# Encoder-decoder layer on one core: the negated maxima of four heads made by one reduction, and the first query block's cross-attention normalization issued in two steps

## The chip, the cores and the metric

The kernel runs on one core of a Trainium2 chip. The core has five engines with a queue of instructions each, worked off in order: TensorE (PE in the profile, its weight loads PEld), VectorE (DVE), ScalarE (ACT), GpSimd (POOL) and SyncE (SP, which here issues the DMAs). The metric is device time in microseconds (us); several runs are given by their median.

## The reference

A pre-norm transformer layer with an encoder over a short context (2 x 77 rows of 512) and a decoder over 2 x 2048 rows of 512; 16 heads of 32, feed-forward width 2048. Cut to what matters:

```
def _mha(xq, xkv, w_in, b_in, w_out, b_out, bias):
    q, k, v = (x @ w.T + b, split into 16 heads of 32)
    scores = q @ k / sqrt(32) + bias[None]          # bias depends on key - query, per head
    attn = softmax(scores, axis=-1)
    return (attn @ v) @ w_out.T + b_out

x = src;  x = x + _mha(ln(x), ln(x), ..., eb);  x = x + relu(ln(x) @ ff1.T + b) @ ff2.T + b   # encoder, 77 rows
memory = x
y = tgt
y = y + _mha(ln(y), ln(y), ..., sb)                 # self attention, causal: 2048 rows see themselves and those before
y = y + _mha(ln(y), memory, ..., cb)                # cross attention: 2048 rows over 77 keys
y = y + relu(ln(y) @ ff1.T + b) @ ff2.T + b         # feed-forward
```

The softmax is computed with each row's maximum taken away before the exponential.

## The kernel before

The decoder rows of a batch b are cut in four blocks m of 512 rows, a block in four query blocks t of 128 rows. There are 4 groups g of 4 heads.

**First half: self attention.** A unit is (b, m, g, t): one query block and the four heads of one group; there are 128, worked in that order. With i = 4m + t a unit has i + 1 key tiles of 128, cut by `pieces` in pieces of up to four tiles. The code is an order written out by hand (the pool has `manual_schedule`): it interleaves, over a stream of pieces, five steps.

- `scores` (line 344): TensorE multiplies q by kT into four PSUM banks, one for each head (line 361). Then DVE goes head by head. Far keys are copied to `pp` with their maximum (line 370); in the last piece of a unit the two tiles at the diagonal get their bias and their maximum (line 377), and a small reduction over the partial maxima makes the negated maximum `nm` of this head (line 384). The exponential of a head (line 387, on ACT, with bias `nm`) is issued at once in block m = 0. In the others it is put in a list, `late_exps`, from which `exps` takes one or two at given places.
- `turn` (line 397): TensorE transposes the exponentials tile by tile (line 411) into PSUM banks; ACT (line 417) and DVE (line 415) copy one half each to `pts`.
- `slot`: the jobs of a unit, which are projections (lines 206, 217, 230, 242), norms, stages of the encoder in the first 30 units or so, and cross attention of the very first block (`first_cross`) in the first units of b = 1.
- `values` (line 422): `pts` times v (line 428).
- `divide`: division by the sums.

PSUM banks are handed out in a ring of seven by `bank()`, whoever asks. A bank is free again when the copy or the pass that reads it is done: a score bank by lines 370 and 377, a transpose's bank by lines 415 and 417. Scores run up to two units ahead of `turn`.

**Second half: cross attention and feed-forward.** For each of the 8 blocks there are 56 slots (`ff_slot`), 28 for each feed-forward layer, which is multiplied by seven products of four slots each. A slot first calls `prepare(s + 3)`, which makes the operand sums (line 1115) for the product three slots later, on POOL in layer 1, into a ring `w_ring` of four buffers; then TensorE multiplies (line 1132 in layer 1, line 1161 in layer 2), and DVE and ACT add the product up (lines 1145, 1147, 1150). Ahead of each slot one step of the generator `cross(x + 1)` runs, that is cross attention of the next block. Its stages come from `attend_stages` (line 754): score (TensorE line 766, DVE lines 773 to 776), exp (ACT line 779), normalize (sums `csu` line 784 and reciprocal `cri` line 785 on DVE, multiply line 786 on POOL), turned (transposes line 792), times_v, out. The places of the stages in `cross` are counted from at = 14 + 7t, by the list at line 1227:

```
for k, f in zip((0 if t else -1, 2 if t else 1, 3 if t else 2, 6, 9, 11), fs):
    plan[at + k].append(f)
```

So for t = 0 score is at slot 13, exp at 15, normalize at 16 and turned at 20.

Of the kernel before, what the change touches and what calls it, by code (L numbers as in the profile page):

```python
# [11 lines left out]
AF = mybir.ActivationFunctionType  # L12
ALU = mybir.AluOpType
AX = mybir.AxisListType
# [3 lines left out]
P = 128  # L18
# [4 lines left out]
HC = P // HD  # L23
# [31 lines left out]
def tile_encoder_decoder(ctx: ExitStack, tc: tile.TileContext, ins, out):  # L55
    nc = tc.nc
# [92 lines left out]
    with (  # L149
# [35 lines left out]
        nTs, qTs, ots, sums_of = {}, {}, {}, {}  # L185
# [151 lines left out]
        late_exps = []  # L337
# [6 lines left out]
        def scores(n, k0, kn):  # L344
            b, m, g, t = units[n]
            i = m * TB + t
            if k0 == 0:
                state[n] = {
                    "p": probabilities(n),
                    "mx": sm.tile([P, HC, 8], F32, name="mx", tag="mx"),  # L350
                    "nm": sm.tile([P, HC], F32, name="nm", tag="nm"),
                    "col": 0,
                }
                if t == 0:
                    sums_of[b, m, g] = sm.tile([P, TB, HC], F32, name="sums", tag="sums")
            st = state[n]
            last = k0 + kn == i + 1
            q = qTs[b, m, g]
            banks = [bank() for _ in range(HC)]
            for r in range(HC):  # L360
                nc.tensor.matmul(  # L361
                    banks[r][:, : kn * P], q[rows4(r), ts(t, P)], kT[rows4(r), g, k0 * P : (k0 + kn) * P],
                    start=True, stop=True,
                )
            far = max(0, kn - 2) if last else kn
            col = st["col"]
            for r in range(HC):
                p, s, c = st["p"][r], banks[r], col
                if far:
                    nc.vector.tensor_scalar(  # L370
                        p[:, k0 * P : (k0 + far) * P], s[:, : far * P], 1.0, None, ALU.mult, ALU.max,
                        accum_out=st["mx"][:, r, c : c + 1],
                    )
                    c += 1
                if last:
                    w = (kn - far) * P
                    nc.vector.tensor_tensor_reduce(  # L377
                        p[:, (i + 1) * P - w : (i + 1) * P], s[:, far * P : kn * P],
                        biases[b, m, g][:, r, 2 * P - w :], 1.0, LOWEST, ALU.add, ALU.max,
                        accum_out=st["mx"][:, r, c : c + 1],  # L380
                    )
                    c += 1
                    nm = st["nm"][:, r : r + 1]
                    nc.vector.tensor_reduce(nm, st["mx"][:, r, :c], AX.X, ALU.max, negate=True)  # L384

                    def run(p=p[:, : (i + 1) * P], nm=nm, to=sums_of[b, m, g][:, t, r : r + 1]):
                        nc.scalar.activation(p, p, AF.Exp, bias=nm, accum_out=to)  # L387

                    if m:
                        late_exps.append((n, run))  # L390
                    else:
                        run()
            st["col"] = c

        got = {}

# [357 lines left out]
        def attend_stages(q, kTc, v, y, biased, pr, pts, place, w_o, bi=None):  # L754


            prh = pr.rearrange("p (h k) -> p h k", k=S)
            by_r = pr.rearrange("p (g r k) -> p g r k", r=HC, k=S)
            keep = {}

            def score():
                mx = sm.tile([P, NC, HC], F32, name="cmx", tag="cmx", bufs=3)
                banks = [bank() for _ in range(HC)]
                for g in range(NC):
                    for r in range(HC):
                        nc.tensor.matmul(  # L766
                            banks[r][:, ts(g, S)], q(g)[rows4(r)], kTc[rows4(r), g, :], start=True, stop=True
                        )
                for r in range(HC):
                    s = banks[r][:, : NC * S].rearrange("p (g k) -> p g k", k=S)  # L770
                    d = by_r[:, :, r, :]
                    if biased:
                        nc.vector.tensor_tensor(d, s, bi[r] if bi else d, ALU.add)
                        s = d
                    nc.vector.tensor_reduce(mx[:, :, r], s, AX.X, ALU.max)
                    nc.vector.tensor_tensor(d, s, mx[:, :, r, None].to_broadcast([P, NC, S]), ALU.subtract)

            def exp():
                nc.scalar.activation(pr, pr, AF.Exp)

            def normalize():
                su = sm.tile([P, H], F32, name="csu", tag="csu", bufs=2)
                ri = sm.tile([P, H], F32, name="cri", tag="cri", bufs=2)
                nc.vector.tensor_reduce(su, prh, AX.X, ALU.add)
                nc.vector.reciprocal(ri, su)
                nc.gpsimd.tensor_tensor(prh, prh, ri[:, :, None].to_broadcast([P, H, S]), ALU.mult)

            def turned():
                for g in range(NC):
                    pt = bank()  # L790
                    for r in range(HC):
                        nc.tensor.transpose(pt[:S, ts(r, P)], prh[:, g * HC + r, :], ident)  # L792
                    if g % 2:
                        nc.vector.tensor_copy(pts(g), pt[:S, :])
                    else:
                        nc.scalar.copy(pts(g), pt[:S, :])

            def times_v():
                ot = bank()
                for g in range(NC):  # L800
                    for r in range(HC):
                        h = g * HC + r
                        nc.tensor.matmul(
                            ot[rows4(r), ts(g, P)], v[:, ts(h, HD)], pts(g)[:, ts(r, P)], start=True, stop=True
                        )
                keep["oT"] = place()
                nc.scalar.copy(keep["oT"], ot)

            def out():
                mm, oT = bank(), keep["oT"]  # L810
                for c in range(NC):
                    nc.tensor.matmul(mm, oT[:, ts(c, P)], w_o[:, c, :], start=(c == 0), stop=(c == NC - 1))  # L812
                nc.vector.tensor_tensor(y(), mm, y(), ALU.add)

            return score, exp, normalize, turned, times_v, out

        def first_cross():

# [40 lines left out]
            for t in range(TB):  # L859
                y = lambda t=t: ys[t]  # L860
                fs = norm_stages(
                    y, "n2", rows["dec_ca_out_b"], lambda: xn, lambda t=t: nT[:, :, ts(t, P)]
                )
# [4 lines left out]
            for t in range(TB):  # L868
                y = lambda t=t: ys[t]
                fs = attend_stages(  # L870
                    lambda g, t=t: qT[:, g, ts(t, P)], kTc, vc, y, t < 2, prs[t % 2], pts, lambda: oT, wo
                )
                for k, f in zip((0, 1, 2, 4, 5, 6), fs):
                    at(11 + 3 * t + k, f)
                fs = norm_stages(y, "n3", rows["dec_ff2_b"], lambda: xn, lambda: slab)
                for k, f in enumerate(fs):
                    at(18 + 3 * t + k, f)

                def store(t=t):
                    nc.sync.dma_start(nT3_d[:, :, ts(t, P)], slab)  # L880
                    nc.sync.dma_start(y1[0][0][:, t, :], ys[t])

                at(20 + 3 * t, store)
# [308 lines left out]
        def cross(x):  # L1192

            b, m = blocks[x]
# [7 lines left out]
            for t in range(TB):  # L1202
                fs = norm_stages(
                    lambda t=t: y_of(x, t), "n2", bv, place("xt"), lambda t=t: nT2[:, :, ts(t, P)]
                )
# [11 lines left out]
            for t in range(TB):  # L1217
                at = 14 + 7 * t
                y = lambda t=t: y_of(x, t)
                biased = m == 0 and t < 2  # L1220
                fs = attend_stages(
                    lambda g, t=t: qT[g // 2][:, g % 2, ts(t, P)], kTcs[b], vcs[b][:S, :], y, biased, pr,
                    lambda g: pts_all[:S, g, :], place("xr"), wbt,
                    bias_1 if biased and t else None,
                )

                for k, f in zip((0 if t else -1, 2 if t else 1, 3 if t else 2, 6, 9, 11), fs):
                    plan[at + k].append(f)
                fs = norm_stages(y, "n3", bo, place("xt"), lambda t=t: nTt[:, :, ts(t, P)])
                for k, f in zip((13, 15, 17), fs):  # L1230
                    plan[at + k].append(f)
# [29 lines left out]
        i = 0  # L1261
        while i < len(stream):
            n = stream[i][0]
# [97 lines left out]
```

## Time and profile before

| | |
|---|---|
| median of 3 runs | 2927.04 us (2926.18 to 2927.46) |
| profiled execution | 2926.58 us, its span 2924.8 us |
| TensorE busy | 2866.0 us, 98% of the span |
| VectorE busy | 2096.9 us, 72% |
| ScalarE busy | 1303.8 us, 45% |
| GpSimd busy | 744.8 us, 25% |
| mean granted TensorE clock | 0.99 |
| line 384 (small reductions) | 512, 156 ns each, 79.8 us |
| line 786 on POOL (multiply of the normalization) | 32, about 2.25 us each |
| end of the self-attention units | about 1765 us |

The page gives for each engine the time with an instruction at work; a group's row gives line, engine, operation, tiles written and read, busy time and mean ns, and the idle time just before it with the work that ended it. Matmuls are pipelined and their ends are modelled, so idle time of TensorE is told by the starts of its matmuls better than by its busy share. In the order of time each row is start, duration, engine, line, operation, and in brackets the idle time before it and who ended that. Times within the execution are counted from the span's start.

### The profile page before, as it was taken

The page shows a single profiled execution, that of the slowest core. Times are in us where ns is not written, and L with a number is a line of the kernel's source. Part 1 is how long each engine was busy: PE and PEld are TensorE (multiplying, and loading weights), DVE is VectorE, ACT ScalarE, POOL GpSimd, SP SyncE. Part 2 cuts the span into 40 slices and gives each one's busy share as a digit, 9 for nine tenths or more (in the row PEclk, how much of TensorE's full clock was granted, in tenths as well). Part 3 has the DMA queues.
Part 4 walks back from the last instruction along what each step waited for, and adds up shares of the span by engine and source line. Part 5 has one row for each costly group of instructions (what it writes and reads, how often), then busy time and mean ns, then how long its engine had stood idle before and what let it go on. Part 6 is the DMA issues. An engine that isn't in the chain of part 4 may idle for free.

```text
span 2924.8 us, 60785 instructions
## 1 busy us (share of the span) xinstructions
PE 2866.0 (98%) x24440; PEld 2018.7 (69%) x24440; DVE 2096.9 (72%) x5951; ACT 1303.8 (45%) x2431; POOL 744.8 (25%) x601
## 2 busy tenths in 40 slices
PE   8899999999999999999999999999999999999999
PEld 5557666666666556666666667777777777777788
DVE  4767688888987788888888894646474756565645
ACT  3344456546665445565566673323232323232321
POOL 0100000000000101000000004565656464646464
PEclk9899999999999999999999999999999999999999
DMA  6413301201111502211201115000001000000000
GB/s 176 98 54 112 100 16 54 65 16 45 34 41 60 141 19 73 73 30 48 56 16 37 41 39 198 1 30 1 29 1 47 1 29 1 30 1 30 1 15 15
DMA packets 117837, 137.11 MB, mean 47 GB/s; under 512 B 18433, under 2 KB 73265, under 8 KB 117427
## 3 DMA queue, kind: packets, MB, share of 16 engines
q1 hardware_dynamic: 117554, 133.22, 15.5%
q8 instruction: 192, 3.15, 0.4%
q14 instruction: 91, 0.74, 0.1%
HBM read 111.33 MB, written 21.86 MB: 46 GB/s over the span
## 4 chain that ended last, share of the span: by engine, by line
PE 86%; DVE 11%; issue 1%; ACT 1%; DMA 1%; POOL 0%; SPq 0%; DVEq 0%; POOLq 0%; ACTq 0%
PE psum L1161 13%; PE psum L1132 13%; PE psum L411 12%; PE psum L361 10%; PE psum L428 7%; DVE pp L370 5%; PE psum L206 4%; PE psum L812 4%; PE psum L751 4%; PE psum L230 4%; PE psum L242 4%; PE psum L217 3%; DVE pp L377 3%; PE psum L792 2%; PE psum L766 1%
## 5 line engine op out<-in xcount | busy, mean ns | idle before, releaser
L387 ACT ACTIVATE pp<-pp,nm 128x128 f32<-128x128 f32 (+15 forms) x512 | 614.1, 1210 | 197.7 <-DVE nm L384 194.9
L370 DVE TENSOR_SCALAR_CACHE_REDUCE pp<-psum 128x512 f32<-128x512 f32 (+3 forms) x1024 | 557.9, 589 | 53.5 <-PE psum L361 51.5
L411 PE MATMUL psum<-ident,pp 128*128 128x128 f32 x4352 | 547.9, 279 | 17.6 <-DVE mx L377 11.7
L411 PEld LDWEIGHTS psum<-ident,pp 128*128 128x128 f32 x4352 | 474.2, 142 | 130.3 <-DVE pp L370 56.5
L417 ACT COPY pts<-psum 128x512 f32<-128x512 f32 (+3 forms) x592 | 298.6, 577 | 516.9 <-PE psum L411 390.9
L1115 POOL TENSOR_TENSOR vv<-pp 128x512 f32<-128x512 f32 x320 | 425.3, 1345 | 148.6 <-PE psum L1132 128.5
L361 PE MATMUL psum<-kT,q 32*128 32x512 f32 (+3 forms) x2560 | 351.8, 579 | 8.2 <-DVE mx L377 4.0
L415 DVE COPY pts<-psum 128x512 f32<-128x512 f32 (+2 forms) x544 | 329.7, 659 | 40.7 <-PE psum L411 38.9
L428 PEld LDWEIGHTS psum<-pts,vv 128*32 128x32 f32 x8704 | 226.2, 110 | 124.3 <-issue 116.9
L428 PE MATMUL psum<-pts,vv 128*32 128x128 f32 x8704 | 278.9, 276 | 0.4 <-DVE vv L233 0.4
L1147 DVE TENSOR_TENSOR kT<-kT,psum 128x512 f32<-128x512 f32 x256 | 166.5, 681 | 133.1 <-PE psum L1132 125.9
L276 POOL TENSOR_TENSOR rstd<-rstd,mhalf 128x1 f32<-128x1 f32 x32 | 18.2, 568 | 918.3 <-DVE rstd L275 855.4
L377 DVE CUSTOM_DVE_ANT_0 pp<-psum,bias 128x256 f32<-128x256 f32 (+1 forms) x512 | 209.4, 409 | 24.6 <-PE psum L361 16.7
L361 PEld LDWEIGHTS psum<-kT,q 32*128 32x128 f32 x2560 | 119.5, 184 | 151.8 <-issue 97.7
L1150 ACT ACTIVATE kT<-kT,vecs 128x256 f32<-128x256 f32 x256 | 115.2, 499 | 196.5 <-DVE kT L1147 196.5
L1161 PE MATMUL psum<-vv 128*128 128x256 f32 x768 | 176.9, 381 | 0.0
L1132 PE MATMUL psum<-oT,vv 128*128 128x256 f32 x736 | 166.8, 380 | 1.5 <-POOL vv L1115 1.5
L1161 PEld LDWEIGHTS psum<-vv 128*128 128x128 f32 x768 | 143.1, 190 | 26.8 <-issue 9.5
L1145 ACT COPY kT<-psum 128x512 f32<-128x512 f32 x124 | 69.5, 587 | 204.4 <-DVE kT L1147 133.8
L1132 PEld LDWEIGHTS psum<-oT,vv 128*128 128x128 f32 x736 | 138.7, 190 | 26.2 <-issue 6.2
L1115 DVE TENSOR_TENSOR vv<-kT 128x512 f32<-128x512 f32 x160 | 131.1, 834 | 17.6 <-PE psum L1161 16.6
L1132 PE MATMUL psum<-nT,vv 128*128 128x256 f32 x512 | 122.0, 389 | 15.1 <-POOL vv L1115 14.6
(176 smaller groups left out, 3870.3 us busy)
## 6 DMA issues: line engine op xcount, KB each, us to landing
wqk<-in_dec_sa_in_wT_dram SPq DMA_DIRECT2D x64, 256.0 KB, 3.7
bias<-tz SPq DMA_DIRECT2D x128, 128.0 KB, 3.6
wbig<-in_dec_sa_in_wT_dram SPq DMA_DIRECT2D x8, 1024.0 KB, 8.5
vv<-in_enc_ff_wT_dram SPq DMA_DIRECT2D x8, 1024.0 KB, 5.7
wbig<-in_dec_sa_out_wT_dram SPq DMA_DIRECT2D x8, 1024.0 KB, 7.7
vv<-y SPq DMA_DIRECT2D x32, 256.0 KB, 3.2
out_dram<-vv SPq DMA_DIRECT2D x32, 256.0 KB, 2.0
xt<-in_x_dram SPq DMA_DIRECT2D x30, 256.0 KB, 3.6
```

What stands on the lines that cost most here:

```text
L361: nc.tensor.matmul(banks[r][:, : kn * P], q[rows4(r), ts(t, P)], kT[rows4(r), g, k0 * P : (k0 + kn) * P], start=True, stop=True,)
L370: nc.vector.tensor_scalar(p[:, k0 * P : (k0 + far) * P], s[:, : far * P], 1.0, None, ALU.mult, ALU.max, accum_out=st["mx"][:, r, c : c + 1],)
L377: nc.vector.tensor_tensor_reduce(p[:, (i + 1) * P - w : (i + 1) * P], s[:, far * P : kn * P], biases[b, m, g][:, r, 2 * P - w :], 1.0, LOW ...
L387: nc.scalar.activation(p, p, AF.Exp, bias=nm, accum_out=to)
L411: nc.tensor.transpose(pt[:, ts(x, P)], state[n]["p"][r][:, ts(k, P)], ident)
L415: nc.vector.tensor_copy(pts[:, : len(load), :], pt[:, :w])
L417: nc.scalar.copy(pts[:, : len(load), :], pt[:, :w])
L428: nc.tensor.matmul(ot[rows4(r), t, :], vv[:, k, ts(g * HC + r, HD)], got.pop((n, k, r)), start=(k == 0), stop=(k == i),)
L1115: engine.tensor_tensor(dst, quarter(*parts[0], n), quarter(*parts[2], n), SIGN[parts[1]])
L1132: nc.tensor.matmul(mm[:, ts(f, TOK)], a[:, c, ts(f, P)], b[:, c, :], start=(c == 0), stop=(c == 1))
L1147: nc.vector.tensor_tensor(dst, dst, got, SIGN[sign])
L1161: nc.tensor.matmul(mm[:, t, :], lhs[:, c, ts(t, P)], rhs[:, c, :], start=(n == 0 and c == 0), stop=(n == 3 and c == 1),)
```

## The change

In `scores` the reduction is taken out of the loop over heads: one `tensor_reduce` over the partial maxima of all four heads writes the four columns of `nm`, behind the last head's passes, and the four exponentials are issued (m = 0) or listed (m > 0) behind it. In `attend_stages` normalize is cut in `sums` (DVE: sums and reciprocal) and `normalize` (POOL: multiply). In `cross` sums and multiply of the first query block are at places 2 and 3 from `at`, where both were at 2; for the other query blocks both stay at 3. In `first_cross` both stay at one place.

```diff
@@ scores
                     c += 1
-                    nm = st["nm"][:, r : r + 1]
-                    nc.vector.tensor_reduce(nm, st["mx"][:, r, :c], AX.X, ALU.max, negate=True)
-
-                    def run(p=p[:, : (i + 1) * P], nm=nm, to=sums_of[b, m, g][:, t, r : r + 1]):
-                        nc.scalar.activation(p, p, AF.Exp, bias=nm, accum_out=to)
-
-                    if m:
-                        late_exps.append((n, run))
-                    else:
-                        run()
             st["col"] = c
+            if not last:
+                return
+
+            nc.vector.tensor_reduce(st["nm"], st["mx"][:, :, :c], AX.X, ALU.max, negate=True)
+            for r in range(HC):
+                p, nm, to = st["p"][r][:, : (i + 1) * P], st["nm"][:, r : r + 1], sums_of[b, m, g][:, t, r : r + 1]
+
+                def run(p=p, nm=nm, to=to):
+                    nc.scalar.activation(p, p, AF.Exp, bias=nm, accum_out=to)
+
+                if m:
+                    late_exps.append((n, run))
+                else:
+                    run()
@@ attend_stages
-            def normalize():
+            def sums():
                 su = sm.tile([P, H], F32, name="csu", tag="csu", bufs=2)
                 ri = sm.tile([P, H], F32, name="cri", tag="cri", bufs=2)
                 nc.vector.tensor_reduce(su, prh, AX.X, ALU.add)
                 nc.vector.reciprocal(ri, su)
+                keep["ri"] = ri
+
+            def normalize():
+                ri = keep["ri"]
                 nc.gpsimd.tensor_tensor(prh, prh, ri[:, :, None].to_broadcast([P, H, S]), ALU.mult)
...
-            return score, exp, normalize, turned, times_v, out
+            return score, exp, sums, normalize, turned, times_v, out
@@ first_cross
-                for k, f in zip((0, 1, 2, 4, 5, 6), fs):
+                for k, f in zip((0, 1, 2, 2, 4, 5, 6), fs):
@@ cross
-                for k, f in zip((0 if t else -1, 2 if t else 1, 3 if t else 2, 6, 9, 11), fs):
+                for k, f in zip((0, 2, 3, 3, 6, 9, 11) if t else (-1, 1, 2, 3, 6, 9, 11), fs):
```

The built program has 384 fewer DVE instructions. On POOL the multiply of the first query block stands one L1115 later in seven blocks; on TensorE, ACT and SP the order is as before.

## The prediction

> **What bounds the kernel now.** I read the busy table first, then the waits, then the order of time at the places that the waits name.
>
> ```profile
> PE 2866.0 (98%) x24440; PEld 2018.7 (69%) x24440; DVE 2096.9 (72%) x5951; ACT 1303.8 (45%) x2431; POOL 744.8 (25%) x601
> ...
> L384 DVE TENSOR_REDUCE nm<-mx 128x1 f32<-128x3 f32 (+4 forms) x512 | 79.8, 156 | 17.8
> ```
>
> TensorE is the bound, so an edit on VectorE (DVE), ScalarE (ACT) or GpSimd (POOL) pays only where TensorE stands still for that engine. The page's "busy" hides short stalls, because a matmul's end is modelled. I therefore took, in the order of time, each matmul's start-to-start distance over the usual one of its pair of forms. Up to 1765 us (self attention) this gives 76 us of TensorE standing for DVE, 53 of it for the release of score banks by line 377. Behind 1765 us it gives 17.3 us for one POOL line. The waits show the same places, with less of their length:
>
> ```profile
> ACT pp L387 <- DVE nm L384: 194.9, 52, 7.9
> ...
> PEld psum L411 <- DVE mx L377: 35.9, 93, 2.2
> ...
> PE psum L1132 <- POOL vv L1115: 16.1, 7, 4.4
> ```
>
> The columns are total us, times, longest. ACT often waits for the negated maximum `nm`; that costs nothing as long as ACT's own readers have slack.
>
> **Part 1: the GpSimd multiply goes behind one operand sum.** The seven waits of 16.1 us are one event in each of blocks 1 to 7, at the first query block:
>
> ```profile
> 1979.73 1.44 DVE L784 TENSOR_REDUCE csu<-oT 128x16 f32<-128x1232 f32 x1 [1.02 <-ACT oT L779]
> 1981.20 0.25 DVE L785 RECIPROCAL cri<-csu 128x16 f32<-128x16 f32 x1
> ...
> 1981.60 2.25 POOL L786 TENSOR_TENSOR oT<-oT,cri 128x1232 f32<-128x1232 f32 x1 [3.99 <-DVE cri L785]
> ...
> 1983.80 1.27 POOL L1115 TENSOR_TENSOR vv<-pp 128x512 f32<-128x512 f32 x1
> ...
> 1985.12 2.66 PE L1132 MATMUL psum<-nT,vv 128*128 128x256 f32 x8 [2.04 <-POOL vv L1115]
> ```
>
> POOL stands 3.99 us for `cri`, multiplies, and only then makes the operand that TensorE is waiting for. In the built order the multiply passes exactly one L1115 in each of seven blocks; `csu` and `cri` keep their place on DVE, no DMA moves, and POOL is the only queue passed. The sum before it ran at 1976.33; the next waits for a ring buffer that TensorE frees one product (1.73 us) later, so it can run at about 1978.1 to 1979.3, inside the idle 3.99 us and 3.6 us before TensorE wants it (1982.9). The multiply still starts at 1981.6, because `cri` sets it. Who is late next: the transposes of slot 20 need the multiply (1983.85), and TensorE comes to them at 1982.9 + 1.73 = 1984.65, so 0.8 us spare. Only block 4, whose score adds a bias, differs: `cri` is ready at 2280.05, the multiply ends at 2282.30, TensorE would be there at about 2280.8. So 1.5 us of its 4.4 stays. The seven waits give 16.1 − 1.5 = 14.6 us.
>
> Three of the seven stalls were followed by a slow clock:
>
> ```profile
> 1985.10:1989.00 3.90, 3.88 (x15) 3.40 (x16) 1.17 (x2) 0.68 (x3) 3.90 (x4) 0.65 0.00 0
> 2283.50:2287.00 3.50, 3.42 (x9) 2.74 (x10) 0.00 (x0) 0.29 (x1) 3.50 (x4) 0.55 0.00 0
> 2433.00:2437.00 4.00, 3.94 (x12) 3.18 (x13) 0.47 (x1) 0.26 (x1) 4.00 (x5) 0.57 0.00 0
> ```
>
> The number before the last two is the granted clock: 0.65, 0.55, 0.57, where the stretches just before have 0.98 to 1.00. Lost: 3.9 x 0.35 + 3.5 x 0.45 + 4.0 x 0.43 = 4.7 us. The Trainium skill, "TensorE: Matmul & The Clock Gate" (HAM oscillation), gives the rule as no idle gap over about 3.4 us; by it only the 4.4 us stall could have cost clock, 1.6 us. The rows show it behind stalls of 2.2 us as well, so I take 4.7. **Part 1: −19.3 us** (by the rule −16.2; bounds −15 and −22).
>
> **Part 2, the gain: three of four small reductions go.** 512 reductions become 128, of 128x4 outputs. Price of one, from the order of time on DVE:
>
> ```profile
> 601.48 0.08 DVE L377 DVE_READ_ACCUMULATOR2_ANT mx<- 128x1 f32 x1
> 601.60 0.16 DVE L384 TENSOR_REDUCE nm<-mx 128x1 f32<-128x4 f32 x1
> 601.67 0.28 DVE L370 TENSOR_SCALAR_CACHE_REDUCE pp<-psum 128x128 f32<-128x128 f32 x1
> 601.88 0.08 DVE L370 DVE_READ_ACCUMULATOR pp<-psum 128x1 f32 x1
> 601.88 0.42 DVE L377 CUSTOM_DVE_ANT_0 pp<-psum,bias 128x256 f32<-128x256 f32 x1
> ```
>
> From the accumulator read to the next head's copy is 601.67 − 601.48 = 0.19 us. Without the reduction the copy may start with the read, as line 377 does behind line 370's read (both 601.88): saved 0.19. If it waits for the read's end, 0.11. The nearest row is 370's, so 0.19; three heads make 0.57 us a unit, less about 0.015 for the wider last reduction (154 to 158 ns for 1 to 5 elements, so some 170 ns for 20). The page "VectorE: DVE Perf Modes" (The DRAIN you can't avoid) speaks against it: the next instruction starts only when the pipe is empty, which is the 0.11 end and would make this gain 16 instead of 27.
>
> What TensorE gets is the smaller of 0.57 and its own stall in that unit. The stalls sit at the third and fourth query block of a group (t = 2, 3), where the last piece still has far keys: typically 0.09 + 0.25 + 0.25 and 0.38 + 0.38. The chain runs through these heads, three `nm` in each such episode. In blocks m = 1 to 3 (48 such units) min(0.57, stall) sums to 26.7 us; other units there have next to no DVE stall. **−27 us** (bounds −12 and −35). It is not lost again: DVE is the later one in these units, and TensorE's path has its own 0.49 us a head beneath DVE's 0.555.
>
> **Part 2, the price: the first exponential waits for all four heads.** `nm` of head 0 now comes with the last, three heads later less 0.55 us: 1.0 us (head period 0.53), 1.7 (0.745) or 2.1 (0.875). The exponentials stand in ACT's queue with the `pts` copies behind them, which free banks and feed the value products.
> - m = 1 and 3 (64 units): ACT comes to the first exponential 0.85 to 2.1 us after its `nm` anyway (behind copies), so it is 0 to 0.8 us late, and the transposes come 2 to 14 us after the exponentials. Exceptions: the first unit of both m = 3 blocks (slack 0.14, delay 0.65) and the last unit (slack 0.14): +2 us.
> - m = 2: in 20 units the first exponential starts 0.03 us after its `nm`. For t = 0, 1, four copies stand right behind it, and the next scores want their banks 0.1 to 0.9 us after a copy's end, against 1.0 us of delay. 12 units, 0.2 to 0.9 each: +6 us. t = 2 has the slack.
> - m = 0 (32 units, exponentials at once): before, ACT worked head by head as DVE did; now the four run after DVE, so they end 3 x E − 0.55 later. E is 0.40, 0.51, 0.62, 0.72 (line 387 by form), so 0.65, 0.97, 1.29, 1.62. TensorE waited for a `pts` copy behind them already in seven units (91, 107, 116, 125, 133, 1024, 1048 us): 2 x 0.65 + 0.97 + 2 x 1.29 + 2 x 1.62 = 8.1. Three more units (50, 141, 178 us) have slack 0.1 to 0.95 against 1.62: 3.6. DVE's own saving where such a wait doesn't cover it: −4.7. **+7 us**; the bounds are 0 (DVE bounds most of 107 to 131 us) and +16 (if longer stalls bring more half-clock stretches; those of 92, 109 to 140 and 1048 us are there now).
>
> **Sum:** −19.3 − 27 + 2 + 6 + 7 = −31.3 us, on the profiled execution's 2926.6 (span 2924.8 and 1.8 around it). The median of the runs is 0.5 higher: 2927.0 − 31.3 = 2895.7, so **2896 us**.
>
> **Rivals.** (a) Self attention gives nothing net: the reductions save the 0.11 end (−16) and the late exponentials cost 15. Then part 1 alone is left: 2927 − 19 = **2908**. For it: 0.1 us of slack in several places. Against it: 10 us of slack in most units. (b) The delay is free nearly everywhere, because TensorE's next wants are set by DVE, which is earlier too: −20 − 35 + 3, **2875**. (c) Slower: the late `nm`. ACT waited for `nm` 52 times; if each passed on 1.3 us (the mean of 1.0 and 1.7) through copies to TensorE, that is +68, against −46: **2949**. It decides from 0.9 us a wait. Against it stand the slacks above, over 3 us for most. (d) The multiply's move does nothing because the ring buffer isn't free earlier and the sum still waits: 2927 − 12 = **2915**. Against it: the sums before it follow each other every 1.73 us as TensorE frees them.
>
> **How the numbers follow.** Likeliest (2896 ± 10): 0.58. (a) 0.20, (b) 0.10, (c) 0.06, (d) 0.06. The range leaves out (c) and the tails of (b) and (d): 2878 to 2915; the likeliest one's own is 2886 to 2906. A change under 0.2% (6 us) can't be told from none here. Slower needs (c): 0.05; within 0.2%, from part of (c): 0.03; faster 0.92.
>
> **What would show it.** In the changed kernel the wait of L1132's line for POOL falls from 16.1 to about 1.5 us and the three slow stretches go; the L377 waits of TensorE fall by half; the reduction shows 128 rows of about 170 ns; ACT's wait for `nm` grows from 195 us and TensorE's wait for `pts` copies grows by about 15 us. It would be wrong if those copy waits grew by 40, or if TensorE waited for ring buffers or L786 in the last half.

## The result, and the profile after

| | before | after |
|---|---|---|
| median of 5 runs each | 2926.99 us (2925.14 to 2927.46) | 2905.19 us (2903.80 to 2908.11) |
| ratio | | 0.9929 (95%: 0.9915 to 0.9944) |
| profiled execution, its span | 2926.58, 2924.8 us | 2908.11, 2906.3 us |

The changed kernel is 21.8 us faster; the forecast was 31.3 us, so 2905 lies inside the range given and 9 us above the predicted time. It lies as near to rival (a), 2908. What follows says which terms were off. The profiled execution of after is the longest of its five; by the spans it is 18.5 us shorter than before, and the comparisons of the two traces add up to that number.

The busy table of after; engine, busy us, share of the span, instructions:

```profile
PE 2860.0 (98%) x24440; PEld 2023.5 (70%) x24440; DVE 2048.5 (70%) x5567; ACT 1299.2 (45%) x2431; POOL 742.7 (26%) x601
```

DVE lost 384 instructions and 48 us of work; TensorE's busy time fell by 6.0 us. TensorE's waits for the `pts` copies before (total us, times, longest):

```profile
PEld psum L361 <- ACT pts L417: 2.6, 13, 0.5
...
PEld psum L546 <- ACT pts L417: 2.2, 2, 1.2
...
PEld psum L766 <- ACT pts L417: 1.2, 1, 1.2
...
PEld psum L576 <- ACT pts L417: 0.6, 1, 0.6
```

The waits of after:

```profile
ACT pp L392 <- DVE nm L387: 264.6, 87, 9.1
...
PEld psum L415 <- DVE mx L377: 12.9, 38, 2.2
PEld psum L361 <- ACT pts L421: 11.0, 30, 2.4
...
PEld psum L550 <- ACT pts L421: 6.1, 2, 3.3
...
PEld psum L580 <- ACT pts L421: 4.1, 2, 2.2
...
PEld psum L770 <- ACT pts L421: 4.0, 2, 3.2
...
PE psum L800 <- POOL oT L794: 1.5, 1, 1.5
...
PEld psum L1140 <- POOL vv L1123: 0.8, 3, 0.4
```

Line 387 is the joint reduction, 392 the exponential, 421 ACT's copy, 794 the POOL multiply, 1123 the operand sums. Three things are to be seen. TensorE's wait for the score banks (line 377) fell from 35.9 to 12.9 us. ACT's wait for `nm` rose from 194.9 in 52 times to 264.6 in 87. And the gap has moved: TensorE stands longer for `pts` copies, at lines 361, 550, 580 and 770 (361, 546, 576 and 766 before). The 16.1 us of TensorE's wait for line 1115 are down to 1.5 us for the multiply and three short weight loads, 0.8 us together.

Where that went in time is told by the start of each block's first pass of line 377, after minus before, as a change within each block of self attention (us). The last column is from the trace's record of the granted clock: us at half speed before 190 us. In m = 0, e1, e3, e4 and e9 have the code of before; how far their entries there stray from 0 is what the same code does from one execution to another.

| kernel | b0 m0 | m1 | m2 | m3 | b1 m0 | m1 | m2 | m3 | half clock to 190 us |
|---|---|---|---|---|---|---|---|---|---|
| before | 0 | 0 | 0 | 0 | 0 | 0 | 0 | 0 | 34.1 |
| cut of the normalization alone (e1) | +0.8 | 0 | 0 | +0.4 | +0.2 | 0 | 0 | 0 | 30.7 |
| after | +11.6 | −4.7 | +3.8 | −5.7 | +0.8 | −5.1 | +2.1 | −2.8 | 47.8 |
| joint reduction alone (e2) | +10.2 | −4.7 | +3.8 | −5.6 | +0.8 | −5.1 | +2.1 | −2.7 | 44.4 |
| joint only in m = 0 (e7) | +9.7 | 0 | 0 | +0.2 | +0.8 | 0 | 0 | +2.3 | 44.4 |
| joint only in m = 1 and 3 (e3) | +0.3 | −5.1 | 0 | −5.6 | +0.4 | −5.1 | 0 | −3.0 | 30.7 |
| head 0 alone, 1 to 3 jointly, m > 0 (e4) | −0.5 | −3.6 | −2.8 | −5.4 | −1.1 | −3.6 | −2.9 | −1.8 | 30.7 |
| e3 with e4's cut in m = 2 (e9) | +0.7 | −5.1 | −2.8 | −5.7 | +0.3 | −5.1 | −2.9 | −4.8 | 30.7 |
| no late exponential (e6) | −4.0 | −3.6 | −2.8 | −5.7 | −2.7 | −3.7 | −2.9 | −3.9 | 27.3 |
| all four reductions kept, late exponentials (e5) | +15.7 | 0 | +12.5 | +0.5 | +6.0 | +0.2 | +12.3 | +3.7 | 44.4 |

In after the self attention comes out at nearly nothing: the first of these passes is 0.7 us later, the eight blocks add up to 0, and the last unit, behind the last pass, adds 1.4. The second half is 20.5 us shorter. So the change's whole gain is its small second part; its large first part gives and takes the same.

### The profile page after: what moved, and what is told of

It reads as the page before. It is cut to its first block, busy times and chain, and to the rows that moved or that the text cites. A ratio compares the mean times of both kernels' runs of the same rounds, so it can differ in the third digit from the quotient of the medians.

```text
span 2906.3 us, 60333 instructions
## 1 busy us (share of the span) xinstructions
PE 2860.0 (98%) x24440; PEld 2023.5 (70%) x24440; DVE 2048.5 (70%) x5567; ACT 1299.2 (45%) x2431; POOL 742.7 (26%) x601
## 3 DMA queue, kind: packets, MB, share of 16 engines
q1 hardware_dynamic: 117554, 133.22, 15.8%
## 4 chain that ended last, share of the span: by engine, by line
PE 93%; DVE 4%; ACT 2%; issue 1%; DMA 1%; POOL 0%; SPq 0%; DVEq 0%; ACTq 0%; POOLq 0%
PE psum L415 17%; PE psum L1169 14%; PE psum L1140 13%; PE psum L361 11%; PE psum L432 8%; PE psum L230 4%; PE psum L206 4%; PE psum L820 4%; PE psum L755 4%; PE psum L242 4%; PE psum L217 3%; PE psum L800 2%; ACT pp L392 1%; PE psum L770 1%; PE psum L811 1%; DVE pp L370 1%
## 5 line engine op out<-in xcount | busy, mean ns | idle before, releaser
L392 ACT ACTIVATE pp<-pp,nm 128x128 f32<-128x128 f32 (+15 forms) x512 | 611.6, 1201 | 264.9 <-DVE nm L387 264.6
L415 PE MATMUL psum<-ident,pp 128*128 128x128 f32 x4352 | 537.7, 278 | 7.8 <-ACT pp L392 3.7
L361 PE MATMUL psum<-kT,q 32*128 32x512 f32 (+3 forms) x2560 | 358.6, 579 | 10.8 <-DVE mx L377 4.0
L377 DVE CUSTOM_DVE_ANT_0 pp<-psum,bias 128x256 f32<-128x256 f32 (+1 forms) x512 | 196.0, 411 | 24.7 <-PE psum L361 16.7
L257 POOL TENSOR_TENSOR xr<-xr,row_dec_sa_out_b 128x512 f32<-128x512 f32 x30 | 38.5, 1285 | 373.3 <-DVE pts L419 242.9
```

Of the source, the lines that this page charges most:

```text
L361: nc.tensor.matmul(banks[r][:, : kn * P], q[rows4(r), ts(t, P)], kT[rows4(r), g, k0 * P : (k0 + kn) * P], start=True, stop=True,)
L377: nc.vector.tensor_tensor_reduce(p[:, (i + 1) * P - w : (i + 1) * P], s[:, far * P : kn * P], biases[b, m, g][:, r, 2 * P - w :], 1.0, LOW ...
L415: nc.tensor.transpose(pt[:, ts(x, P)], state[n]["p"][r][:, ts(k, P)], ident)
```

## The experiments

**Each part alone.** The change is taken apart. e1 is the kernel before with the edits of `attend_stages`, `first_cross` and `cross` alone, e2 is the kernel before with the edit of `scores` alone.

> The kernel before with the cross-attention part alone: sums and multiply in two steps, the reductions one for each head as before. My theory (the seven waits of TensorE for the operand sum, 16.1 us less 1.5, and the slow clock behind three of them, 4.7): -19 to -21 us, about 2906.5 against 2927. The time of the changed kernel, 2905, would then be nearly all from here. Rival, that the self-attention part gives the 12 us that I forecast for it and this one only the rest: -10 us, 2917.

> The kernel before with the self-attention part alone: one reduction for the four heads in every block, cross attention as before. My forecast had -27 for the gain and +15 for the price, 2915. The trace of the changed kernel says otherwise (blocks m = 1 and 3 about -4 to -5 us each, m = 2 about +2 to +4 each, m = 0 about +12 and +1): 2926 to 2930, within what can be told from no change.

Measured beside a before of 2927.6: e1 2907.2 us, ratio 0.9932 (0.9918 to 0.9947); e2 2926.5 us, ratio 0.9999 (0.9989 to 1.0008). The cut alone gives 20.4 us, the joint reduction alone 1.1 us, which its interval does not tell from nothing. Together that is 21.5 of the 21.8 us, so no interaction of the parts shows. And e2's blocks are those of after, within 0.1 us but for the first: the zero is made of gains of 10 and 8 us a batch in m = 1 and 3, and of losses in m = 0 and 2.

**Where the joint reduction pays.** A list of groups of heads says which maxima are made together and when their exponentials are issued or listed. e3 and e4 are after with other groups, e7 is before with them, e9 is after with both groupings. In the cut below `GROUPS` stands for each run's list.

```diff
-            nc.vector.tensor_reduce(st["nm"], st["mx"][:, :, :c], AX.X, ALU.max, negate=True)
+                    for a, e in GROUPS:      # EACH = (0, 1), (1, 2), (2, 3), (3, 4)
+                        if r == e - 1:
+                            maxima(n, a, e, c)   # reduces heads a to e-1, then their exponentials
# e3: ((0, 4),) if m in (1, 3) else EACH
# e4: ((0, 1), (1, 4)) if m else EACH
# e7: ((0, 4),) if m == 0 else EACH          (and the normalization as before)
# e9: ((0, 4),) if m in (1, 3) else ((0, 1), (1, 4)) if m else EACH
```

> The split of cross attention as in the changed kernel, one reduction for four heads in blocks m = 1 and 3 only, one for each head in m = 0 and 2. Theory (three reductions less are worth 0.56 us in a unit where VectorE is what TensorE waits for; the late first exponential costs only where ScalarE is ready for it, in m = 0 and 2): -20.5 - 2 x 5 - 2 x 4 = about -38, 2888. Rival (what the blocks show is chance of the clock, the reductions are worth nothing): 2906.

> The split as in the changed kernel; in blocks m = 1 to 3 head 0 has a reduction of its own and heads 1 to 3 one together, in m = 0 one for each head. Theory (the price comes from head 0's maximum being late; ScalarE needs 1.2 us or more for head 0, so the other three are ready in time): two reductions less instead of three, 0.37 us a unit, without the price: m = 1 and 3 some -3 us a block, m = 2 some -2.5 a block, with the split -20.5 - 12 - 5 = about -37, 2890. Rival (the price comes from the other heads too): m = 2 stays at +3 a block, 2900.

> The kernel before with one reduction for four heads in the blocks m = 0 alone, cross attention as before. Theory: the price there, +10 to +12 in the first batch's block and +1 in the second's, about half of it half-clock stretches of TensorE: 2938. My forecast's size for it: +7, 2934. Rival, that the first block's time varies by itself: 2927 +- 3.

> The split; the joint reduction in m = 1 and 3, head 0 apart and three together in m = 2, one for each head in m = 0. If the blocks add up as the runs so far show them (split -20.5; joint: m = 1 -5.1 twice, m = 3 -5.6 and -3; apart: m = 2 -2.8 twice): 2927.6 - 44.9 = 2883 (2880 to 2887), a little under the kernel with head 0 apart everywhere (2885.1).

| | us | ratio to before |
|---|---|---|
| e3 | 2889.4 (2889.3 to 2889.9) | 0.9872 (0.9855 to 0.9888) |
| e4 | 2885.1 (2885.0 to 2887.0) | 0.9858 (0.9843 to 0.9873) |
| e7 | 2939.6 (2935.5 to 2939.7) | 1.0037 (1.0021 to 1.0053) |
| e9 | 2882.3 (2881.7 to 2882.9) | 0.9846 (0.9829 to 0.9862) |

Leaving m = 0 and m = 2 as they were (e3) makes the changed kernel 15.8 us faster. Only m = 0 joined (e7) makes the kernel before slower, by 10.5 us in the two m = 0 blocks; 2.3 more are in the last block, where its code is that of before. Setting head 0 apart in m = 2 (e9 against e3) turns a change of 0 into −5.6 us there, where the full join has +5.9: the same instructions saved but one, and 11.5 us between them. Counted unit by unit, 10.4 of these are lost at twelve places of the kind that follows, where e4 loses nothing, and 1.6 go with a half-clock stretch that stands behind one of them; less 0.4 that the join gains elsewhere. The two differ there only in how head 0's maximum is made.

Three kernels at one place, the first query block of a group in m = 2. The order of time before, then after, then e4; start, duration, engine, line, work, in brackets the idle time before:

```profile
449.29 0.16 DVE L384 TENSOR_REDUCE nm<-mx 128x1 f32<-128x3 f32 x1
449.48 1.26 ACT L387 ACTIVATE pp<-pp,nm 128x1152 f32<-128x1152 f32 x1 [2.95 <-DVE nm L384]
...
450.73 2.02 ACT L417 COPY pts<-psum 128x512 f32<-128x512 f32 x4
...
453.13 1.14 PE L361 MATMUL psum<-kT,q 32*128 32x512 f32 x8
```

After:

```profile
456.91 0.17 DVE L387 TENSOR_REDUCE nm<-mx 128x4 f32<-128x12 f32 x1
457.11 1.26 ACT L392 ACTIVATE pp<-pp,nm 128x1152 f32<-128x1152 f32 x1 [3.98 <-DVE nm L387]
...
458.37 2.03 ACT L421 COPY pts<-psum 128x512 f32<-128x512 f32 x4
...
459.73 1.85 PE L361 MATMUL psum<-kT,q 32*128 32x512 f32 x8
...
460.45 0.30 PEld L361 LDWEIGHTS psum<-kT,q 32*128 32x128 f32 x4 [0.20 <-ACT pts L421]
```

e4, with head 0 apart:

```profile
444.13 0.16 DVE L391 TENSOR_REDUCE nm<-mx 128x1 f32<-128x3 f32 x1
444.33 1.26 ACT L396 ACTIVATE pp<-pp,nm 128x1152 f32<-128x1152 f32 x1 [2.94 <-DVE nm L391]
...
445.58 2.03 ACT L425 COPY pts<-psum 128x512 f32<-128x512 f32 x4
...
447.99 1.14 PE L361 MATMUL psum<-kT,q 32*128 32x512 f32 x8
```

ACT stands idle until this exponential, and four copies are queued behind it. Before, the copies ended at 452.75 and TensorE wrote its next eight scores from 453.13: 0.38 us to spare. After, ACT's idle time is 1.03 us longer (3.98 for 2.95), the copies end at 460.40, and the eight scores take 1.85 us for 1.14, because the second four wait for a copy (last row): 0.71 us, near the delay less its spare, 0.65. In e4 the wait is 2.94 again and the eight take 1.14.

**Gain and price apart.** e5 keeps the four small reductions beside the joint one, so DVE saves nothing, and the exponentials come later still than in after: at the place shown ACT's idle time is 4.60 us, 0.62 more than the 3.98 of after. e6 takes three of four reductions out and delays nothing.

```diff
@@ e5: after, with, behind each head's passes
+                    nc.vector.tensor_reduce(st["own"][:, r : r + 1], st["mx"][:, r, :c], AX.X, ALU.max, negate=True)
@@ e6: before with the cut normalization, and
-                    nm = st["nm"][:, r : r + 1]
-                    nc.vector.tensor_reduce(nm, st["mx"][:, r, :c], AX.X, ALU.max, negate=True)
+                    nm = st["nm"][:, 0:1]
+                    if r == 0:
+                        nc.vector.tensor_reduce(nm, st["mx"][:, r, :c], AX.X, ALU.max, negate=True)
```

> The changed kernel, but the four small reductions of the heads are made as well, into a tile that nobody reads; the exponentials still wait for the joint one. So the late maximum stays and is 0.55 us later still, and the gain is gone: 640 reductions. Theory: blocks m = 1 and 3 about 0 to +3 us each against the kernel before, m = 2 +8 to +12 each (measured +3.8 and +2.1 with the gain of some 3 in them), m = 0 +15 to +25 and +1 to +5; with the split's -20.5 some 2940 to 2955. Rival, that the late maximum is harmless and the changed kernel's m = 0 and 2 are the clock's doing: 2907 to 2912.

> The split as in the changed kernel; head 0's negated maximum, made right behind head 0's passes, is the bias of all four exponentials, and the other three reductions are left out. A row's softmax doesn't depend on what is taken away before the exponential as long as nothing overflows, so all of the layer is computed. The gain without the price: an exponential waits for its own head's scores and for head 0's maximum. Theory: -0.56 us in the units t = 2 and 3 of m = 1 and 3 as in the changed kernel (-5 and -4 a block), m = 2 -4 a block, m = 0 0 to -5; -20.5 - 10 - 8 - 8 - 3, about 2877 (2870 to 2884).

Measured beside a before of 2927.5: e5 2957.0 us, ratio 1.0101 (1.0080 to 1.0121); e6 2876.9 us, ratio 0.9827 (0.9813 to 0.9842). With the price alone the self attention loses some 50 us against e1, 2 us more than the range expected of e5; with the gain alone it wins 30. The two don't add up to after's nothing, as e5's delay is the longer one. In e5 the blocks m = 1 and the first m = 3 hardly change, so there the delay is free even without the gain; nearly all of it falls on m = 0 and m = 2 (and part on the last block). The waits of e5 (total us, times, longest) name the same two consumers:

```profile
ACT pp L394 <- DVE nm L389: 319.9, 112, 9.6
...
PEld psum L362 <- ACT pts L423: 19.3, 44, 2.7
...
PE psum L552 <- ACT pts L423: 5.9, 2, 3.2
```

Against those of e6:

```profile
ACT pp L388 <- DVE nm L385: 197.8, 51, 7.9
...
PEld psum L361 <- ACT pts L418: 3.4, 13, 1.1
...
PE psum L547 <- ACT pts L418: 1.7, 2, 0.9
```

Line 362 and line 361 are the scores, 552 and 547 a stage of the encoder. The wait of ACT is back at before's 195 us and the copies' waits with it.

**Versions that beat both.** e4 and e9 take each head's own maximum and are 20 and 23 us faster than the changed kernel. e6 is 28 us faster than it; the maximum that it takes away is that of the group's first head, which leaves a softmax unchanged but bounds the exponent of the other three heads no longer by their own maximum.

## Why the prediction was right, and where its sizes were off

The number is right because part 1 was sized right and the range took in rival (a). The −12 us forecast for the joint reduction did not come: e2 gives 1.1 us, not told from nothing. So 2905 lies at the edge of the likeliest case's own 2886 to 2906, but by its mechanism it is rival (a)'s result, to which the forecast gave 0.20; that it fell inside the likeliest 10 us as well is luck.

**Part 1, −19.3 forecast, −20.4 (e1) and −20.5 (second half of after) measured: right in its steps.** The order of time of after at the place shown before:

```profile
1978.02 7.07 PE L1140 MATMUL psum<-nT,vv 128*128 128x256 f32 x32
1978.33 1.28 POOL L1123 TENSOR_TENSOR vv<-pp 128x512 f32<-128x512 f32 x1 [0.45 <-PE psum L1140]
...
1981.48 0.25 DVE L789 RECIPROCAL cri<-csu 128x16 f32<-128x16 f32 x1
...
1981.88 2.25 POOL L794 TENSOR_TENSOR oT<-oT,cri 128x1232 f32<-128x1232 f32 x1 [2.27 <-DVE cri L789]
...
1984.93 1.91 PE L800 MATMUL psum<-ident,oT 128*77 128x128 f32 x16
```

The sum runs at 1978.33, in the forecast's span of 1978.1 to 1979.3, inside POOL's old idle time; the multiply still starts when `cri` is there; the four products of line 1140 run without a stall, and the transposes come 0.8 us behind the multiply. Rival (d), a ring buffer that isn't free, is out. Block 4, for which 1.5 us were to stay:

```profile
2274.67 2.25 POOL L794 TENSOR_TENSOR oT<-oT,cri 128x1232 f32<-128x1232 f32 x1 [5.69 <-DVE cri L789]
...
2276.97 1.97 PE L800 MATMUL psum<-ident,oT 128*77 128x128 f32 x16 [1.49 <-POOL oT L794]
```

1.49 us. The three half-clock stretches at 1986, 2283 and 2433 us are gone too; after shows none between 1525 us and its last microseconds. The page "TensorE: Matmul & The Clock Gate" (HAM oscillation) with its 3.4 us of idle time ascribes only one of them to its stall, which made the part −16.2; the rows of 0.55 to 0.65 behind all three made it −19.3, and −20.4 was measured. The two stretches behind stalls of some 2 us went with their stalls. Which of those stalls is followed by a stretch is not fixed, though: e2 and e7 still have all seven stalls, with stretches behind the 4.4 us one (6.8 us) and behind one of 2.0 us in block 7 (3.4 us), where before has none. In all three runs it is 10.2 us at half clock.

**Part 2, the gain of 27: right.** The order of time on DVE after:

```profile
612.68 0.08 DVE L377 DVE_READ_ACCUMULATOR2_ANT mx<- 128x1 f32 x1
612.68 0.29 DVE L370 TENSOR_SCALAR_CACHE_REDUCE pp<-psum 128x128 f32<-128x128 f32 x1
...
613.23 0.08 DVE L377 DVE_READ_ACCUMULATOR2_ANT mx<- 128x1 f32 x1
613.23 0.28 DVE L370 TENSOR_SCALAR_CACHE_REDUCE pp<-psum 128x128 f32<-128x128 f32 x1
...
614.34 0.08 DVE L377 DVE_READ_ACCUMULATOR2_ANT mx<- 128x1 f32 x1
...
614.46 0.17 DVE L387 TENSOR_REDUCE nm<-mx 128x4 f32<-128x16 f32 x1
```

The next head's copy starts with the accumulator's read, so the 0.19 us end holds and a head takes 0.555 us for 0.745. The 0.11 us end, for which the prediction named the page "VectorE: DVE Perf Modes" (The DRAIN you can't avoid), does not: by it a unit would gain 0.33 us. The prediction left out that the same section goes on to except a next instruction that is not held back, which may start earlier; the rows show one that starts with the read. Measured from one unit's first transposes to the next's, 30 of the 32 waiting units of m = 1 and 3 gain 0.52 to 0.69 us each, nearly all of them 0.56; in m = 2 it is 0.26 and 0.35 to 0.56. There e4, with one reduction more, gains the same in all but one of these units a batch, so TensorE's stall was the smaller term. All shortened units of m = 1 to 3 add up to 9.9 + 10.2 + 5.7 = 25.8 us.

**The price in m = 1 and 3, +2: right in kind, small.** Gains of 20.1 us there, and a net of 9.9 + 8.4 = 18.3 by the table, less the last unit's 1.4 behind it, 16.9: a price of 3.2 us. Part of it is the clock: after has a half-clock stretch of 6.8 us at 1518 us, in the last block, and before has none there; e7, with before's code in that block, has one at 1526 us and is 2.3 us longer there. In the first m = 3 block it is the other way: before has such a stretch at 652 us, after none, and that is some of the gain counted there.

**The price in m = 2, +6: the first size that was off, measured +12.** The step was "12 units, 0.2 to 0.9 each". Twelve it was: the trace has the lateness at the same place of each group, between 0.67 and 1.05 us, 10.4 in all, and once there was a stretch at half clock behind it (3.41 us from 538 us, 1.6 us more). I had written the mechanism and the 1.0 us of delay, and then taken the middle of the slacks. Half of the places had no slack at all and passed on the whole 1.03; the others lost 0.67 to 0.72. e5 confirms it: its delay is 0.62 longer, and the same places, those with a half-clock stretch apart, lose 1.65 and 1.29 to 1.33.

**The price in m = 0, +7 with a bound of +16: the second, measured +12.3.** The four exponentials come one behind another after the last head, as forecast. One of the seven places, the one at 91 us, from the unit's first pass on DVE on, before and then after:

```profile
87.17 0.29 DVE L370 TENSOR_SCALAR_CACHE_REDUCE pp<-psum 128x128 f32<-128x128 f32 x1 [3.58 <-PE psum L361]
...
88.04 0.62 ACT L387 ACTIVATE pp<-pp,nm 128x384 f32<-128x384 f32 x1 [1.02 <-DVE nm L384]
...
90.87 0.62 ACT L417 COPY pts<-psum 128x256 f32<-128x256 f32 x2
...
91.28 0.78 PE L546 MATMUL psum<-pp 32*77 32x77 f32 x26 [0.83 <-ACT pts L417]
```

```profile
89.83 0.29 DVE L370 TENSOR_SCALAR_CACHE_REDUCE pp<-psum 128x128 f32<-128x128 f32 x1 [3.59 <-PE psum L361]
...
92.37 0.61 ACT L392 ACTIVATE pp<-pp,nm 128x384 f32<-128x384 f32 x1 [2.69 <-DVE nm L387]
...
94.78 0.62 ACT L421 COPY pts<-psum 128x256 f32<-128x256 f32 x2
...
95.18 1.32 PE L550 MATMUL psum<-pp 32*77 32x77 f32 x26 [2.63 <-ACT pts L421]
```

From the first row to ACT's copies it is 3.70 us before and 4.95 after: 1.25 us later, where the forecast's 3 x E − 0.55 gives 1.29 for exponentials of 0.62 us. TensorE's wait grew by 1.80 us, because DVE's saving brings it there 0.56 us earlier; its 26 products start 1.24 us later. So the lateness had the size forecast here. But these products then take 1.32 us for 0.78: in after the clock stands at half from 94.6 to 101.5 us. That term is also in the windows, where the last number but two is the granted clock. The first 190 us before:

```profile
0.00:190.00 190.00, 172.70 (x1151) 100.47 (x1151) 122.04 (x463) 69.32 (x196) 18.07 (x25) 0.91 0.44 112
```

and after:

```profile
0.00:190.00 190.00, 165.07 (x1028) 95.59 (x1028) 105.01 (x375) 59.11 (x182) 16.47 (x24) 0.87 0.42 108
```

Half clock for 47.8 us instead of 34.1 is at most 13.7 x 0.5 = 6.9 us of TensorE's work. Two units have most of the first batch's loss, which from first transposes to first transposes is 11.4 us: 2.63 in the one from 87.4 us on, with 3.4 us more at half clock than before, and 4.67 in the one from 137.0, with 5.8 us more. e5, whose delay is longer, has 1.6 us less at half clock than before in the second of them and loses only 2.15 there. The second batch has the same code in its units, no encoder between its scores, and +0.8. The forecast gave "longer stalls bring more half-clock stretches" as the reason of its upper bound and left it out of its value.

How much of the price is the clock stays an estimate. What a stretch costs can be read where the code is the same. One unit of the second batch's m = 0 took 13.15 us in e4, with 3.4 us at half clock, and 14.35 to 14.71 with 6.8 us in before, e1, e3 and e9. But in the first batch's m = 0, e1, e3, e4 and e9 had 3.4 us less than before and differed from it by −0.5 to +0.8 us. So a us at half clock cost from nothing to nearly half a us. Nor is it shown that the stalls bring the stretches: e7 and e2 show both growing (44.4 us, +10 us) and e6 both falling (27.3 us, −4.0), but e5 has e2's 44.4 us with +15.7, and after, with e2's code there, has 47.8 with +11.6.

**The sum.** Part 1 −20.5, gain −25.8, prices 3.2 + 12.0 + 12.3 = 27.5: −18.8, for the 18.5 us between the two spans (the median of after is 2.9 us below its profiled execution). The 12 us by which the forecast missed in self attention are the prices in m = 2 and m = 0: 24.3 for 13. The reason that rival (a) gave was only half right too, since the reductions did not save the 0.11 end but the 0.19, and the late exponentials cost not 15 but 28, the clock's part included. Of the signs listed, the wait for POOL and the reduction's row (157 to 176 ns) came as said; the wait for line 377 fell to a third, not to a half; and the waits of TensorE's weight loads for `pts` copies, all lines together, rose from 6.6 to 29.5 us, by 23 where 15 was said and 40 would have been a refutation. Rival (c) needed 0.9 us a wait at every place where ACT waits; e5 shows such a price in m = 2, but m = 1 and most of m = 3 pass nothing on.

## What to carry to other kernels

Four results made at once save the producer three instructions and make the first consumer wait for the other three results; count the waits of the consumer that stands idle for the first result, and price each with the whole delay unless a row shows a spare. That gives the 10.4 us of m = 2 here; it does not give the half-clock stretches. Set the first result apart where the consumer is idle and join the rest, as e4 does. In an in-order queue, let a ready instruction pass one that must wait anyway, as in part 1.

## What the runs showed that was not expected

The same edit cost 11.6 us in one batch's first block and 0.8 in the other's. What differs is the encoder work between the scores, where the waits for copies at lines 550 and 580 are, and the clock, which was already going down there; no run separates these two. And the single reduction of head 0 that e4 and e6 keep shows in m = 1 as 0.38 us a unit instead of 0.56, that is 0.18 for one small reduction, at TensorE's position and not only on DVE's.
